# Perceiver layer on one core: self attention regrouped from one pair of heads per step to two pairs per stage

## The chip, the cores and the metric

One core of a Trainium2 chip runs the whole layer. The metric is device time in microseconds (us) of one execution. The kernel before takes 757.04 us, the median of three runs (756.72 to 757.04).

The engines are called as the profile calls them: PE (matmuls), PEld (weight loads for them), DVE and ACT (element by element work, both read the matmul results in PSUM), POOL (element by element work in SBUF) and SP (issues most DMAs). Each engine runs its own instructions in order; they wait for one another through semaphores.

## The reference

The layer is three residual blocks over x (256 tokens of 512):

```
x = x + cross_attention(layernorm(x), ctx_1024)      # 25088 context rows
x = x + self_attention(layernorm(x))                 # 16 heads of 64, one shared k and v, causal
x = x + mixture_of_experts(layernorm(x))             # 64 experts, 8 per token
```

The change touches the second block alone:

```
xn = layernorm(x);  q = xn w_q^T;  k, v = split(xn w_kv^T)
sim[h] = q[h] k^T * scale, masked causally;  attn[h] = softmax(sim[h])
out = concat_h(attn[h] v) w_out^T;  return layernorm(out)
```

Everything is 32 bit float.

## The kernel before

The 256 tokens are two tiles of 128 (`t`, `kt` = 0, 1; NT = 2). Width 512 is four chunks of 128 (ND = 4). The 16 heads are eight pairs `e` = 0..7 (NE = 8), because two heads of 64 fill 128 partitions. Cross attention takes the first 550 us or so, the experts begin at about 612 us; between them lies the self attention, of which the eight pairs take from 566.9 to 604.1 us.

What one pair needs:

- `queries(e)` (L907): eight matmul instructions (four chunks, two passes each) of 128x256 on all 128 rows and columns of the array, into a PSUM bank (`pa`), and one copy that scales the result into `aq`. The copy is on DVE for e = 1, 2, 3, otherwise on ACT (L925 to L928). For e = 0, 1 and half of 2 the queries lie before the loop.
- `scored(e)` (L998): eight matmul instructions for the scores `ps`. Each contracts 64 rows, the two heads side by side on the upper and lower half of the rows of the array. Then, on DVE, the causal mask is added (L1019, two additions) and the negated row maxima are found (L1023, two reductions).
- `exponential(e, t)` (L1027): ACT takes the exponential with the row sums, four activations for a pair, into `pe`.
- `divided(e, t)` (L1041): three reciprocals on DVE, three multiplications on POOL (L1049).
- `turned(e)` (L1055): six transposes on PE (`ptp`, on the whole array) and two copies out of PSUM: `pT0` (128x512, on DVE) and `pT1` (128x256, on ACT or DVE).
- `weighted(e)` (L1083): eight matmul instructions with 64 output columns each, the two heads on the left and right half of the columns of the array (`po`), and a copy of the result to `oT` on ACT. The last pair does this by halves of the tokens.
- `project` (L979): the output projection `pw`, two instructions of 128x512 for each token tile and pair, on the whole array. Some of them are used as fillers in the loop (`fill`).

So PE works in three arrangements of its array here: whole (queries, transposes, projection), two halves of rows (scores) and two halves of columns (products with the values).

The loop (L1123) is a pipeline over `e`: step e turns pair e - 2, divides pair e - 1, computes queries for a later pair (from step 6 on: two projections), scores pair e, weighs pair e - 2, and takes the exponentials of pair e. On PE a steady step is therefore transposes, queries, scores, products, each for one pair.

The order of the work is written out by hand: `in_turn` keeps the marked instructions of each engine in the order of the program. PSUM has eight banks. The two score tiles `ps` share four of them (`banks`, two buffers of two banks), so the scores of pair e + 2 wait until the exponentials of pair e have been read. `keys_bank`, `scores_bank`, `third_bank` and `apart` are one bank each; `among_three` goes round the first three of these.

After the loop the remaining projections follow (L1183 to L1189). When `pw` of the first token tile is complete, DVE and ACT compute its layer norms (`attended(0)`) while PE does six projections of the second tile.

Of the kernel before, what the change touches and what calls it, by code (L numbers as in the profile page):

```python
# [11 lines left out]
AF = mybir.ActivationFunctionType  # L12
# [3 lines left out]
P = 128  # L16
# [6 lines left out]
def tile_perceiver_layer(  # L23
# [25 lines left out]
    nc = tc.nc  # L49

    T, D = x.shape
# [3 lines left out]
    DH = a_wkvT.shape[1] // 2  # L55
# [4 lines left out]
    NT = T // P  # L60
    ND = D // P
# [4 lines left out]
    NE = INNER // P  # L66
# [26 lines left out]
    in_turn = tc.keep_in_program_order  # L93
# [112 lines left out]
    def keep_warm(*widths):  # L206
# [44 lines left out]
        fill=NEG,  # L251
# [269 lines left out]
    for i in range(2):  # L521
        t = cpool.tile([P, NT_SUMS, WIDTH + 2], F32, tag=f"T{i}", name=f"T_{i}", bufs=1)
# [125 lines left out]
    before, named = None, Named(0)  # L648
    for g in range(G):
# [25 lines left out]
        before, named = named, Named(g + 1)  # L675
# [26 lines left out]
    for line in RESULTS.strip().splitlines():  # L702
        to, x_, op, y_ = line.split()
        a_, b_, o_ = result(x_), result(y_), result(to)
        n = widths[to] = min(widths[x_], widths[y_])
        assert to not in ("c01", "c11") or n == WIDTH
        if to[0] == "c" and to[2] != "1":
            n = WIDTH - 2
        f = nc.vector.tensor_add if op == "+" else nc.vector.tensor_sub
# [78 lines left out]
    def among_three(name):  # L788
        turns[0] += 1
        return (keys_bank, scores_bank, third_bank)[turns[0] % 3](name)  # L790
# [113 lines left out]

    begun = {}

    def queries(e, lo=0, hi=T, where=apart, chunks=range(ND)):  # L907

        if chunks[0] == 0:
            begun[e, lo] = where(f"pa_{e}_{lo}")  # L910
        pa = begun[e, lo]
        for c in chunks:
            in_turn(
                nc.tensor.matmul(  # L914
                    pa[:, 0 : hi - lo],
                    lhsT=a_wqT_sb[:, c, e * P : (e + 1) * P],
                    rhs=anT[:, c, lo:hi],
                    start=(c == 0),
                    stop=(c == ND - 1),
                )  # L920
            )
        if chunks[-1] < ND - 1:
            return
        to, src = aq[:, e, lo:hi], pa[:, 0 : hi - lo]
        if 0 < e < 4:  # L925
            in_turn(nc.vector.tensor_scalar(to, src, 1.0 / DH, None, ALU.mult))
        else:
            in_turn(nc.scalar.activation(to, src, AF.Copy, scale=1.0 / DH))  # L928


    vT = hpool.tile([P, T], F32, tag="vT", name="vT")
# [62 lines left out]
    def fill(n):  # L994
        for _ in range(n):
            project(*fillers.pop(0))

    def scored(e):  # L998

        ps = banks(f"ps_{e}")  # L1000
        parts = []
        for t in range(NT):
            nk = (t + 1) * P
            lo = t * P
            parts.append(ps[:, :, lo : lo + nk])
            for i in range(2):
                half = slice(i * DH, (i + 1) * DH)
                in_turn(
                    nc.tensor.matmul(  # L1009
                        ps[:, i, lo : lo + nk],  # L1010
                        lhsT=aq[half, e, t * P : (t + 1) * P],
                        rhs=kk[half, 0:nk],
                        start=True,
                        stop=True,
                    )
                )
        for t, sc in enumerate(parts):
            diagonal = sc[:, :, t * P : (t + 1) * P]
            in_turn(nc.vector.tensor_add(diagonal, diagonal, tri))  # L1019
        maxima = []  # L1020
        for t, sc in enumerate(parts):
            nmx = small.tile([P, 2], F32, tag="nmx", name=f"nmx_{e}_{t}")
            in_turn(nc.vector.tensor_reduce(nmx, sc, AX.X, ALU.max, negate=True))  # L1023
            maxima.append(nmx)
        return parts, maxima, []

    def exponential(e, t):  # L1027
        parts, maxima, found = scores_of[e]
        nm = f"{e}_{t}"
        pe = work_b.tile([P, 2, (t + 1) * P], F32, tag=f"pe{t}", name=f"pe_{nm}", bufs=3)  # L1030
        sums = small.tile([P, 2, 1], F32, tag="sums", name=f"sums_{nm}")
        for i in range(2):
            in_turn(
                nc.scalar.activation(
                    pe[:, i, :], parts[t][:, i, :], AF.Exp, bias=maxima[t][:, i : i + 1],
                    accum_out=sums[:, i, :],
                )
            )
        found.append((pe, sums))

    def divided(e, t):  # L1041

        pe, sums = scores_of[e][2][t]
        rs = small.tile([P, 2, 1], F32, tag="rsm", name=f"rsm_{e}_{t}")

        n = 2 - t
        for i in range(0, 2, n):
            in_turn(nc.vector.reciprocal(rs[:, i : i + n], sums[:, i : i + n]))
            nc.gpsimd.tensor_mul(  # L1049
                pe[:, i : i + n],  # L1050
                pe[:, i : i + n],
                rs[:, i : i + n].to_broadcast([P, n, (t + 1) * P]),
            )

    def turned(e):  # L1055


        found = [pe for pe, _ in scores_of.pop(e)[2]]
        done = []
        pts = [among_three(f"ptp_{e}_{kt}") for kt in range(NT)]  # L1060

        for t, i, kt in ((0, 0, 0), (0, 1, 0), (1, 0, 0), (1, 0, 1), (1, 1, 0), (1, 1, 1)):
            o = i * (NT - kt) * P + (t - kt) * P
            in_turn(
                nc.tensor.transpose(  # L1065
                    pts[kt][:, o : o + P], found[t][:, i, kt * P : (kt + 1) * P], ident
                )
            )
        for kt, pt in enumerate(pts):
            n = (NT - kt) * P  # L1070
            pT = work_b.tile([P, 2, n], F32, tag=f"pT{kt}", name=f"pT_{e}_{kt}")
            to = pT.rearrange("p i q -> p (i q)")
            if kt == 1 and e < 2:

                copies_left.append((to, pt[:, : 2 * n]))
            elif kt == 0 or e == NE - 2:
                in_turn(nc.vector.tensor_copy(to, pt[:, : 2 * n]))
            else:
                in_turn(nc.scalar.copy(to, pt[:, : 2 * n]))
            done.append(pT)  # L1080
        return done

    def weighted(e, done):  # L1083


        if e == NE - 1:

            for t in range(NT):
                po = among_three(f"po_{e}_{t}")
                for kt in range(t + 1):  # L1090
                    for i in range(2):
                        in_turn(
                            nc.tensor.matmul(
                                po[i * DH : (i + 1) * DH, 0:P],
                                lhsT=va[:, kt, :],
                                rhs=done[kt][:, i, (t - kt) * P : (t - kt + 1) * P],
                                start=(kt == 0),
                                stop=(kt == t),
                            )
                        )  # L1100
                in_turn(nc.scalar.copy(oT[:, e, t * P : (t + 1) * P], po[:, 0:P]))
            return
        po = among_three(f"po_{e}")
        for kt, pT in enumerate(done):
            for i in range(2):
                in_turn(
                    nc.tensor.matmul(
                        po[i * DH : (i + 1) * DH, kt * P : T],
                        lhsT=va[:, kt, :],
                        rhs=pT[:, i, :],  # L1110
                        start=(kt == 0),
                        stop=(kt == NT - 1),
                    )
                )
        in_turn(nc.scalar.copy(oT[:, e, :], po[:, :T]))

    scores_of = {}
    copies_left = []  # L1120
    queries(1, P, T, where=among_three)
    turn_values()
    for e in range(NE + 2):  # L1123
        done = None
        if e == 1:
            queries(e + 1, P, T)
        if e == 2:
            queries(e + 2)
        if e == 3:
            queries(e + 2, chunks=range(ND // 2))  # L1130
        if e == NE + 1:
            fill(1)
        if e - 2 in scores_of:
            done = turned(e - 2)
        if e - 1 in scores_of:
            divided(e - 1, 0)
            for each in copies_left:
                in_turn(nc.vector.tensor_copy(*each))
            copies_left.clear()
            divided(e - 1, 1)  # L1140
        if e == 1:
            queries(e + 2, where=among_three)
        elif e == 3:
            queries(e + 2, chunks=range(ND // 2, ND))
        elif 2 < e < NE - 2:
            queries(e + 2)
        if e >= NE - 2:
            fill(2 if e <= NE else 1)
        if e < NE:
            scores_of[e] = scored(e)  # L1150
        if done is not None:
            weighted(e - 2, done)
        if e < NE:
            for t in range(NT):
                exponential(e, t)


    fn = work.tile([P, NT, D], F32, tag="tok", name="fn")
# [825 lines left out]
```

## Time and profile before

| what | us |
|---|---|
| median of three runs | 757.04 |
| the profiled execution's own time | 757.02 |
| its span, first to last instruction | 755.2 |
| PE busy in the span | 749.6 |
| the eight pairs, from the transposes of the values ahead of the first scores to the first projection behind the loop | 566.91 to 604.08 |
| the same stretch: DVE busy / ACT busy / POOL busy in 583.16 to 591.54 (8.38 long) | 5.96 / 5.25 / 3.51 |

The span is counted from the first to the last instruction; the 1.8 us by which the time exceeds it lie outside. Busy times of matmuls overlap, since each starts before the one ahead of it has ended; the distance from start to start tells what one costs. The granted PE clock is 1.00 of full speed in each stretch of the attention.

### The profile page before, as it was taken

The numbers are of one execution on the slowest core, as the hardware profiler recorded it, in microseconds if no ns is written. First come the engines' busy times: TensorE is split into PE (matmuls) and PEld (weight loads), VectorE is DVE, ScalarE is ACT, GpSimd is POOL, SyncE is SP. The second block draws the span as 40 slices with busy tenths as digits, with TensorE's granted clock in tenths as the row PEclk, the third lists the DMA queues.
The fourth block names the chain that finished last, engine by engine and source line by source line (L and its number), as shares of the span: only waits on it lengthen the run. The fifth ranks groups of instructions, "written<-read, shape, count | busy, mean of one in ns | idle before, by whom it ended". The sixth has DMA issues, their size and how long they took to land.

```text
span 755.2 us, 12461 instructions
## 1 busy us (share of the span) xinstructions
PE 749.6 (99%) x4046; PEld 614.8 (81%) x4046; DVE 571.6 (76%) x1644; ACT 200.9 (27%) x484; POOL 209.2 (28%) x402
## 2 busy tenths in 40 slices
PE   9999999999999999999999999999999999999998
PEld 6888888888888888888888888888977578876775
DVE  6988887888888788788878878888677669432465
ACT  4222222222222222222222222222244540001110
POOL 3222232232222223223222222322213315430461
PEclk9999999999999999999999999999999999999999
DMA  9999998997876887787788778774051007998552
GB/s 249 268 242 262 293 223 255 255 219 186 214 188 172 214 194 175 193 210 184 176 215 193 171 202 203 179 184 110 1 197 55 2 29 277 388 355 320 174 162 86
DMA packets 156147, 148.64 MB, mean 197 GB/s; under 512 B 8310, under 2 KB 113923, under 8 KB 156080
## 3 DMA queue, kind: packets, MB, share of 16 engines
q1 hardware_dynamic: 153168, 140.28, 70.5%
q0 software_dynamic: 2240, 7.02, 3.0%
q8 instruction: 33, 0.54, 0.3%
q10 hardware_dynamic: 672, 0.52, 0.2%
q14 instruction: 34, 0.28, 0.1%
HBM read 145.63 MB, written 2.16 MB: 196 GB/s over the span
## 4 chain that ended last, share of the span: by engine, by line
PE 99%; DVE 1%; ACT 0%; issue 0%
PE xacc L593 38%; PE pk L372 22%; PE pz L392 11%; PE ph_e L1263 7%; PE seven L1380 4%; PE pa L914 2%; PE ph_s L1263 2%; PE pw L983 2%; PE ph_few L1755 2%; PE po_few L1786 1%; PE ph_first L1263 1%; PE ph_second L1263 1%; PE pd_last L1448 1%; PE ptp L1065 1%; PE ps L1009 1%; PE py L757 1%
## 5 line engine op out<-in xcount | busy, mean ns | idle before, releaser
L593 PE MATMUL xacc<-T,S 128*128 128x172 f32 (+2 forms) x912 | 185.5, 308 | 0.0
L372 PE MATMUL pk<-cT,wkT_sb 128*128 128x384 f32 x512 | 175.5, 486 | 0.0
L593 PEld LDWEIGHTS xacc<-T,S 128*128 128x128 f32 x912 | 152.5, 190 | 20.1
L372 PEld LDWEIGHTS pk<-cT,wkT_sb 128*128 128x128 f32 x512 | 97.1, 190 | 54.4
L560 POOL TENSOR_TENSOR T<-ctx 128x172 f32<-128x172 f32 x65 | 31.8, 490 | 386.6 <-PE xacc L593 375.9
L336 DVE STREAM_TRANSPOSE cT<-quarters 128x1536 f32<-128x1536 f32 x64 | 113.5, 1774 | 0.5 <-issue 0.5
L560 DVE TENSOR_TENSOR T<-ctx 128x172 f32<-128x172 f32 (+1 forms) x262 | 113.5, 434 | 0.0
L560 DVE TENSOR_TENSOR S<-zT 128x128 f32<-128x128 f32 x196 | 57.1, 292 | 71.1 <-ACT zT L401 71.1
L392 PE MATMUL pz<-qT,kT 128*128 128x256 f32 x392 | 106.1, 379 | 0.0
L401 ACT ACTIVATE zT<-pz 128x256 f32<-128x256 f32 (+1 forms) x131 | 64.2, 490 | 113.7 <-PE pz L392 113.7
L593 PE MATMUL xacc<-T,zT 128*128 128x173 f32 (+1 forms) x396 | 89.9, 308 | 0.0
L593 PE MATMUL xacc<-ctx,S 128*128 128x172 f32 x392 | 78.5, 309 | 0.0
L383 ACT ACTIVATE kT<-pk,bk 128x384 f32<-128x384 f32 (+2 forms) x68 | 38.4, 568 | 146.8 <-PE pk L372 146.8
L560 DVE TENSOR_TENSOR S<-zT,S 128x128 f32<-128x128 f32 x325 | 76.6, 285 | 0.0
L570 ACT COPY T<-ctx 128x170 f32<-128x170 f32 (+1 forms) x130 | 43.2, 334 | 124.9 <-PE xacc L593 120.6
L560 POOL TENSOR_TENSOR T<-ctx,T 128x170 f32<-128x170 f32 (+1 forms) x130 | 72.4, 574 | 0.0
L560 DVE TENSOR_TENSOR T<-ctx,T 128x172 f32<-128x172 f32 x195 | 65.4, 361 | 8.2 <-PE xacc L593 1.5
L392 PEld LDWEIGHTS pz<-qT,kT 128*128 128x128 f32 x392 | 68.5, 190 | 3.8 <-ACT kT L383 0.2
L593 PEld LDWEIGHTS xacc<-T,zT 128*128 128x128 f32 x396 | 66.4, 190 | 0.3
L593 PEld LDWEIGHTS xacc<-ctx,S 128*128 128x128 f32 x392 | 62.8, 190 | 0.1
L593 PE MATMUL xacc<-ctx,zT 128*128 128x170 f32 (+1 forms) x264 | 59.5, 307 | 0.0
L1263 PE MATMUL ph_e<-fT,gu 128*128 128x256 f32 x224 | 50.3, 381 | 0.0
(310 smaller groups left out, 791.4 us busy)
## 6 DMA issues: line engine op xcount, KB each, us to landing
ctx<-in_context SPq DMA_DIRECT2D x65, 768.0 KB, 5.3
quarters<-in_context SPq DMA_DIRECT2D x256, 192.0 KB, 6.4
gu<-in_e_gate_up SPq DMA_DIRECT2D x12, 1024.0 KB, 8.1
gu_s<-in_s_gate_up SPq DMA_DIRECT2D x8, 512.0 KB, 6.5
dn<-in_e_down SPq DMA_DIRECT2D x7, 512.0 KB, 6.8
a_wqT<-in_a_wqT SPq DMA_DIRECT2D x4, 512.0 KB, 7.5
a_wout<-in_a_woutT SPq DMA_DIRECT2D x1, 2048.0 KB, 10.4
dn_s<-in_s_down SPq DMA_DIRECT2D x4, 512.0 KB, 8.8
```

Of the source, the lines that this page charges most:

```text
L336: in_turn(nc.vector.transpose(new_turned(g), q.rearrange("p b (c r) -> p c b r", r=R)))
L372: nc.tensor.matmul(pk, lhsT=w[:, c, :], rhs=cT[:, c, 0 : n // R, :].rearrange("p b r -> p (b r)"), start=(c == 0), stop=(c == ND - 1),)
L383: in_turn(nc.scalar.activation(kT[:, lo:hi], pk[:, lo:hi], AF.Identity, bias=bk_sb))
L392: nc.tensor.matmul(pz[:, i * T : (i + 1) * T], lhsT=kT[:, at : at + P], rhs=qT, start=True, stop=True,)
L401: nc.scalar.activation(zT[:, blocks[0] : blocks[-1] + 1, :].rearrange("p j t -> p (j t)"), pz[:, 0 : len(blocks) * T], AF.Sigmoid, scale=1 ...
L560: in_turn(f(o_, a_, b_))
L570: in_turn(nc.scalar.copy(named[to][:, 0:n], named[x_][:, 0:n]))
L593: nc.tensor.matmul(banks_of_products[i][:, cols], lhsT=named[lhs], rhs=named[rhs][:, 0:n],  start=i not in opened, stop=(g == G - 1 and last),
L914: nc.tensor.matmul(pa[:, 0 : hi - lo], lhsT=a_wqT_sb[:, c, e * P : (e + 1) * P], rhs=anT[:, c, lo:hi], start=(c == 0), stop=(c == ND - 1),)
L983: nc.tensor.matmul(pw[t], lhsT=oT[:, e, t * P : (t + 1) * P], rhs=a_wout_sb[:, e, :], start=(e == 0), stop=(e == NE - 1),)
L1263: nc.tensor.matmul(ph[:, f * T + lo : f * T + hi], lhsT=gu[:, c, col : col + P], rhs=fT[:, c, lo:hi], start=(c == 0), stop=(c == ND - 1),)
L1380: nc.tensor.matmul(product_of_seven(nm), lhsT=block(n, hT, dn, s_, t_, lhs), rhs=block(n, hT, dn, s_, t_, rhs),  start=(n == SEVEN[0] and ...
```

## The change

The loop goes over stages `d` = 0..4 instead of steps. A stage scores two pairs, 2d and 2d + 1, one behind the other; then it turns the first pair of the stage before, computes queries (or projections), turns the second pair of the stage before, computes queries again, and forms the products with the values for both of these pairs, one behind the other. The amount of matmul work is the same.

- `queries` is split: the matmuls, and `queries_copied`, which is placed later. In the loop the copies are all on ACT; before, those for e = 2 (second half) and 3 were on DVE.
- `scored` is split: the matmuls, and `masked`, the masks and maxima on DVE.
- `turned` is told which banks to use and which copies are ACT's (`by_act`). `pT1` is always ACT's (before, for e = 0, 1 and 6, DVE's), and for e = 1, 3 and 5 `pT0` is ACT's as well.
- `weighted` is told its banks; the copy to `oT` is split off (`output_copied`) and placed behind the exponentials of the stage's second pair.
- The divisions of the first pair are in its own stage, those of the second pair at the end of the stage.
- Seven projections are in the loop as fillers instead of eight; the eighth follows behind it.
- Fixed banks take the place of `among_three` in the loop.

```diff
-        if 0 < e < 4:
-            in_turn(nc.vector.tensor_scalar(to, src, 1.0 / DH, None, ALU.mult))
-        else:
-            in_turn(nc.scalar.activation(to, src, AF.Copy, scale=1.0 / DH))
+        if by_act:
+            in_turn(nc.scalar.activation(to, src, AF.Copy, scale=1.0 / DH))
+        else:
+            in_turn(nc.vector.tensor_scalar(to, src, 1.0 / DH, None, ALU.mult))
...
+    half = ND // 2
+    queries_of = (
+        ([(2, P, T, keys_bank), (3, 0, T, apart)], [(4, 0, T, third_bank)]),
+        ([(5, 0, T, apart)], [(6, 0, T, keys_bank, range(half))]),
+        ([(6, 0, T, keys_bank, range(half, ND))], [(7, 0, T, apart)]),
+    )
+
+    def ahead(d, j):
+        if d < len(queries_of):
+            for e, lo, hi, *where in queries_of[d][j]:
+                chunks = where[1] if len(where) > 1 else range(ND)
+                queries(e, lo, hi, where[0], chunks, copied=False)
+        elif d == len(queries_of):
+            fill(2)
+        else:
+            fill(2 - j)
...
+    for d in range(NE // 2 + 1):
+        now = [e for e in (2 * d, 2 * d + 1) if e < NE]
+        before = (2 * d - 2, 2 * d - 1) if d else ()
+        free = apart if d == 2 else keys_bank
+        done = {}
+        for e in now:
+            scored(e)
+        if now:
+            masked(now[0])
+        if before:
+            done[before[0]] = turned(before[0], (free, scores_bank), (1,))
+        if now and not before:
+            exponential(now[0], 0)
+            exponential(now[0], 1)
+            ahead(d, 0)
+            masked(now[1])
+            divided(now[0], 0)
+            divided(now[0], 1)
+            ahead_copied(d, 0)
+            ahead(d, 1)
+        else:
+            for t in range(NT if now else 0):
+                exponential(now[0], t)
+            ahead(d, 0)
+            if now:
+                masked(now[1])
+                divided(now[0], 0)
+                divided(now[0], 1)
+            done[before[1]] = turned(
+                before[1], (third_bank, scores_bank), (0, 1) if now else (1,)
+            )
+            ahead_copied(d, 0)
+            ahead(d, 1)
+            weighted(before[0], done[before[0]], third_bank)
+            if now:
+                weighted(before[1], done[before[1]], scores_bank)
+            else:
+                output_copied(before[0])
+                weighted(before[1], done[before[1]], scores_bank, keys_bank)
+        if now:
             for t in range(NT):
-                exponential(e, t)
+                exponential(now[1], t)
+            ahead_copied(d, 1)
+            for e in before:
+                output_copied(e)
+            divided(now[1], 0)
+            divided(now[1], 1)
```

More of the change, by code (lines that the diff above doesn't have):

```diff
@@ L905, in tile_perceiver_layer, with queries @@
     begun = {}
-    def queries(e, lo=0, hi=T, where=apart, chunks=range(ND)):
+    def queries(e, lo=0, hi=T, where=apart, chunks=range(ND), copied=True):
         if chunks[0] == 0:
@@ L921, in queries, with queries_copied @@
             )
-        if chunks[-1] < ND - 1:
-            return
-        to, src = aq[:, e, lo:hi], pa[:, 0 : hi - lo]
-        if 0 < e < 4:
+        if chunks[-1] == ND - 1 and copied:
+            queries_copied(e, lo, hi, by_act=e == 0)
+    def queries_copied(e, lo=0, hi=T, by_act=True):
+        to, src = aq[:, e, lo:hi], begun.pop((e, lo))[:, 0 : hi - lo]
+        if by_act:
+            in_turn(nc.scalar.activation(to, src, AF.Copy, scale=1.0 / DH))
+        else:
             in_turn(nc.vector.tensor_scalar(to, src, 1.0 / DH, None, ALU.mult))
-        else:
-            in_turn(nc.scalar.activation(to, src, AF.Copy, scale=1.0 / DH))
     vT = hpool.tile([P, T], F32, tag="vT", name="vT")
@@ L1016, in scored, with masked @@
                 )
+        scores_of[e] = parts, [], []
+    def masked(e):
+        parts, maxima, _ = scores_of[e]
         for t, sc in enumerate(parts):
@@ L1019, in scored @@
             in_turn(nc.vector.tensor_add(diagonal, diagonal, tri))
-        maxima = []
         for t, sc in enumerate(parts):
@@ L1024, in scored @@
             maxima.append(nmx)
-        return parts, maxima, []
     def exponential(e, t):
@@ L1053, in divided, with turned @@
             )
-    def turned(e):
+    def turned(e, where, by_act):
         found = [pe for pe, _ in scores_of.pop(e)[2]]
         done = []
-        pts = [among_three(f"ptp_{e}_{kt}") for kt in range(NT)]
+        pts = [where[kt](f"ptp_{e}_{kt}") for kt in range(NT)]
         for t, i, kt in ((0, 0, 0), (0, 1, 0), (1, 0, 0), (1, 0, 1), (1, 1, 0), (1, 1, 1)):
@@ L1072, in turned, with weighted @@
             to = pT.rearrange("p i q -> p (i q)")
-            if kt == 1 and e < 2:
-                copies_left.append((to, pt[:, : 2 * n]))
-            elif kt == 0 or e == NE - 2:
+            if kt in by_act:
+                in_turn(nc.scalar.copy(to, pt[:, : 2 * n]))
+            else:
                 in_turn(nc.vector.tensor_copy(to, pt[:, : 2 * n]))
-            else:
-                in_turn(nc.scalar.copy(to, pt[:, : 2 * n]))
             done.append(pT)
         return done
-    def weighted(e, done):
-        if e == NE - 1:
+    def weighted(e, done, *where):
+        if len(where) == NT:
             for t in range(NT):
-                po = among_three(f"po_{e}_{t}")
+                po = where[t](f"po_{e}_{t}")
                 for kt in range(t + 1):
@@ L1102, in weighted @@
             return
-        po = among_three(f"po_{e}")
+        po = where[0](f"po_{e}")
         for kt, pT in enumerate(done):
@@ L1114, in weighted, with output_copied @@
                 )
-        in_turn(nc.scalar.copy(oT[:, e, :], po[:, :T]))
+        outputs[e] = po
+    def output_copied(e):
+        in_turn(nc.scalar.copy(oT[:, e, :], outputs.pop(e)[:, :T]))
+    outputs = {}
     scores_of = {}
-    copies_left = []
     queries(1, P, T, where=among_three)
     turn_values()
[L1123 to L1153, printed above, removed]
-            for t in range(NT):
-                exponential(e, t)
@@ new lines, in ahead_copied @@
+    def ahead_copied(d, j):
+        if d < len(queries_of):
+            for e, lo, hi, *where in queries_of[d][j]:
+                if len(where) == 1 or where[1][-1] == ND - 1:
+                    queries_copied(e, lo, hi)
+    for d in range(NE // 2 + 1):
[34 more added lines that the diff above has]
+                weighted(before[1], done[before[1]], scores_bank)
+            else:
+                output_copied(before[0])
+                weighted(before[1], done[before[1]], scores_bank, keys_bank)
+        if now:
+            for t in range(NT):
+                exponential(now[1], t)
[4 more added lines that the diff above has]
+            divided(now[1], 1)
```

## The prediction

> **What bounds it now.** I read the page first, its chain that ended last and the busy times, then the stretch of the eight pairs: busy times window by window, the order of time on PE, on ACT and on DVE.
>
> ```profile
> PE 749.6 (99%) x4046; PEld 614.8 (81%) x4046; DVE 571.6 (76%) x1644; ACT 200.9 (27%) x484; POOL 209.2 (28%) x402
> PE 99%; DVE 1%; ACT 0%; issue 0%
> 574.14:578.87 4.73, 4.50 (x32) 2.96 (x31) 3.94 (x11) 3.02 (x15) 1.76 (x3) 1.00 0.01 3
> 578.87:583.16 4.29, 4.29 (x31) 3.03 (x30) 3.33 (x10) 2.77 (x14) 1.75 (x3) 1.00 0.01 2
> 587.36:591.54 4.18, 4.18 (x28) 2.30 (x27) 2.98 (x8) 2.63 (x13) 1.75 (x3) 1.00 0.00 0
> ```
>
> The first two lines are the page's: PE is the whole chain. The others are steps of the loop, from one pair's first score to the next one's: length, then busy us of PE, PEld, DVE, ACT, POOL, the granted clock, DMA. A steady step is 4.18 (PE full, ACT 2.63, DVE 2.98, no DMA). The steps from 574.14 and 578.87 hold the same PE work and take 0.55 and 0.11 more: waits. So only PE time can be won: by fewer waits, or by cheaper matmuls. The second is in the order of time on PE (start, length, instructions, count):
>
> ```profile
> 586.83 0.59 PE L914 MATMUL pa<-anT,a_wqT 128*128 128x256 f32 x2
> 587.05 0.38 PE L914 MATMUL pa<-anT,a_wqT 128*128 128x256 f32 x1
> 587.36 0.38 PE L1009 MATMUL ps<-kk,aq 64*128 64x128 f32 x2
> 587.68 0.60 PE L1009 MATMUL ps<-kk,aq 64*128 64x256 f32 x4
> 587.90 0.38 PE L1009 MATMUL ps<-kk,aq 64*128 64x256 f32 x2
> 588.21 0.44 PE L1107 MATMUL po<-pT,va 128*64 128x256 f32 x2
> 588.48 0.49 PE L1107 MATMUL po<-pT,va 128*64 128x256 f32 x4
> 588.80 0.28 PE L1107 MATMUL po<-pT,va 128*64 128x128 f32 x2
> 589.01 0.33 PE L1065 MATMUL ptp<-ident,pe 128*128 128x128 f32 x1
> 589.18 0.49 PE L1065 MATMUL ptp<-ident,pe 128*128 128x128 f32 x3
> ```
>
> Read starts, not lengths. 256 wide matmuls follow at 0.22 (586.83, 587.05; 587.68, 587.90), 128 wide ones at 0.11. Whenever the arrangement of the array changes (128*128, 64*128, 128*64), the last instruction before lasts 0.09 to 0.10 longer (587.05 to 587.36 is 0.31; 587.90 to 588.21 is 0.31; 588.80 to 589.01 is 0.21), and the first one after also: scores 0.10 (587.36 to 587.68 is 0.32 for two that need 0.22), products 0.05 (588.21 to 588.48), transposes 0.06 (589.01 to 589.18), other whole-array matmuls 0.10 (604.08 to 604.61). A steady pair pays three changes: 0.09+0.10+0.09+0.05+0.10+0.06 = 0.49 of its 4.18.
>
> **The change, part by part.**
>
> *Two pairs side by side.* Changes in the loop before: whole to rows 8, rows to whole 2, rows to columns 6, columns to whole 8, whole to columns 2: 26. After: stage 0 into and out of the scores 2; stages 1 to 3 each into scores, out to transposes, into products 9; out of the products of stage 3, into and out of those of stage 4, 3: 14. Leaving: 26 x 0.095 = 2.47 becomes 1.33. Entering scores: 8 x 0.10 becomes 4; entering columns: 8 x 0.05 becomes 4; entering whole: 5 x 0.06 and 5 x 0.10 become 4 x 0.06 and 2 x 0.10. Together 4.47 becomes 2.37: **-2.1**. Columns straight to rows is not in the trace; between 0.14 and 0.20 a change, I take 0.195, as whole to rows costs.
>
> [...]
>
> *Old waits of PE.* The excess of the two early steps, 0.55+0.11, less 0.04 for a dearer entry (queries behind products instead of transposes): **-0.6**. They are waits for `pT1` and `aq` 4, queued behind exponentials, and for POOL. After, stage 1's products come four microseconds behind its transposes, and nothing waits there.
>
> *The copies moved to ACT, and the copies placed later.* No PE time of their own; hidden if ACT keeps up. Its rows:
>
> ```profile
> 588.33 0.90 DVE L1019 TENSOR_TENSOR ps<-ps,tri 128x256 f32<-128x256 f32 x2 [0.20 <-PE ps L1009]
> 589.26 1.02 DVE L1023 TENSOR_REDUCE nmx<-ps 128x2 f32<-128x256 f32 x2
> 590.40 0.37 ACT L1034 ACTIVATE pe<-ps,nmx 128x128 f32<-128x128 f32 x1 [0.90 <-DVE nmx L1023]
> 592.00 0.38 ACT L1079 COPY pT<-ptp 128x256 f32<-128x256 f32 x1
> 610.83 0.59 ACT L308 COPY fT<-pt_fn 128x512 f32<-128x512 f32 x1 [1.75 <-PE pt_fn L298]
> ```
>
> Masks and maxima of a pair take 1.95 (588.33 to 590.28), 0.12 later its exponentials start and hold ACT 1.60 (590.40 to 592.00; last sum at 592.12). ACT is idle 0.90 before them.
>
> What is late next is the second pair's score bank: it is free only after that pair's exponentials, and these stand on ACT behind the first pair's exponentials and three copies. The ring, exponentials of one second pair to those of the next: reciprocal 0.27 (they stand on DVE ahead of the next masks), masks 1.95, 0.12, exponentials 1.60, `pT0` on ACT 0.59 (the only 128x512 copy of ACT is `fT`), `pT1` 0.26, one `aq` 0.29, exponentials 1.72: **6.8**. PE's stage: two steady pairs less one set of changes, 8.38 - 0.49 = 7.89 in stage 3; stages 1 and 2 hold 12 query instructions instead of 16, 0.86 less: 7.03. So ACT is hidden by 0.2 at the tightest, and by 1.1 in stage 3.
>
> *New waits.* In stage 0 there is no cover. Placed on the times of before: masks of pair 0 end at 569.95, those of pair 1 at 571.8; the exponentials of pair 0 end at 571.76, then `aq` 2 and 3 (0.2+0.29), so those of pair 1 run from 572.2 to 573.95. PE: scores of pair 1 end at 568.5, queries 2 (half), 3, 4 take 0.9+0.1+1.73+1.73, so scores 2 start at 573.05, scores 3 could at 573.9: wait 0.1. In stage 4 the transposes of pair 6 use the scores bank, free after the copy of `oT` 5, which stands behind the last exponentials: 0.2. Scores 7 wait for `aq` 7, copied behind the exponentials of pair 5: just in time. Bounds: 0.1 (only stage 0), and 1.2 if every handover to scores 3, 5, 7 is 0.3 later. I take **+0.3**.
>
> *Moved work.* The eighth filler projection goes behind the loop, same PE time; it covers the copy of `oT` 7. Six projections still cover `attended(0)` (fn is done at 609.86, PE turns it at 610.19). No DMA is issued in the loop, so SP passes nothing. Division of second pairs: POOL's 1.75 must end 3.9 later, before the second transposes; covered by the scores, transposes and queries between.
>
> **Sum.** -2.1 - 0.6 + 0.3 = -2.4 in the pairs' 37.2. Behind them PE is busy 131.7 of 135.0, and what feeds it follows from the routing, which comes 2.4 earlier as well; so it passes to the end. The profiled execution goes from 757.02 (span 755.2) to 754.6; the median shown, 757.04, is the same within 0.02: **754.6**.
>
> **Rivals.**
>
> 1. *The changes cost what they cost* (no saving): the loss belongs to the first weights of each block, not to the array's arrangement, and comes again between the two pairs' blocks. For: each block has its own stationary operand. Against: within a block of scores or products weights change as well, without loss. Then -0.6+0.3: 756.7. 12%.
> 2. *Slower, ACT and DVE as the bound.* [...] The place: the ring above. Each us that it exceeds PE's stage is paid at scores 3, 5 and 7. From (2.4 + 0.3) / 3 = 0.9 on nothing is left of the gain, from 1.4 per handover the kernel is over 1.5 slower; at 1.7 it is 759.4. Against: ACT is busy 5.25 of 8.38 now, and with `pT0` 5.84 of 7.0. 8%.
> 3. *Part of the gain eaten*: the 0.2 of cover is gone and each handover waits 0.4, or the experts' stage gives some back: 755.9. 12%.
>
> **Numbers.** My forecast has 68%, with its own range 753.9 to 755.5 (new waits 0.1 to 1.2). A measurement can tell 0.2%, 1.5 us, from no change: faster is below 755.5. Faster: 0.68 and a third of rival 3, 0.72; within: 0.18; slower: 0.10, rival 2 and what I haven't seen. The range leaves out rival 2 and the edges: 753.8 to 756.8.
>
> **What would show it.** PE's order of time: scores of two pairs joined at 0.21, without 0.31; 14 changes. PE's waits: one of about 0.1 at scores 3, one at the transposes of pair 6. Loop end near 601.7 instead of 604.08. Wrong if scores 5 or 7 wait for exponentials by over 0.5, if the joint of two score blocks costs 0.2, or if the experts' stage is longer than before.

## The result, and the profile after

The kernel after takes 754.78 us (median of 9 runs, 754.40 to 755.27) against 756.90 (9 runs): a ratio of 0.9971, 95% interval 0.9961 to 0.9981, so faster by 2.1 us, 0.3%. 754.6 was forecast.

The page of the kernel after, line 1 and the chain that ended last:

```profile
PE 746.8 (99%) x4046; PEld 615.0 (82%) x4046; DVE 566.2 (75%) x1636; ACT 203.0 (27%) x492; POOL 208.5 (28%) x402
PE 98%; DVE 1%; DMA 0%; ACT 0%; issue 0%
```

PE is still the chain, with the same 4046 matmuls, and it is busy 2.8 us less. None was taken away, so they follow one another sooner. How much of that is cheaper changes of the arrangement and how much shorter waits, the starts tell.

The stages 1, 2 and 3, from the first score of a stage to what follows its products (length, then busy us of PE, PEld, DVE, ACT, POOL, granted clock, DMA):

```profile
572.90:580.04 7.14, 7.14 (x58) 5.46 (x57) 4.98 (x16) 5.40 (x24) 3.94 (x8) 1.00 0.01 2
580.04:587.06 7.02, 7.02 (x59) 5.54 (x57) 4.97 (x15) 5.31 (x23) 3.29 (x7) 1.00 0.01 2
587.06:594.98 7.92, 7.92 (x55) 4.69 (x53) 5.29 (x17) 6.13 (x25) 4.37 (x9) 1.00 0.01 3
```

7.03, 7.03 and 7.89 were forecast. ACT is busier in a stage than before (5.3 of 7.0), but not full.

The order of time on PE where stage 2 begins (start, length, instructions, count). Neighbouring windows of the trace overlap, so a line may repeat an instruction of the one above; read the starts:

```profile
579.83 0.28 PE L1108 MATMUL po<-pT,va 128*64 128x128 f32 x2
580.04 0.38 PE L1012 MATMUL ps<-kk,aq 64*128 64x128 f32 x2
580.36 0.60 PE L1012 MATMUL ps<-kk,aq 64*128 64x256 f32 x4
580.58 0.49 PE L1012 MATMUL ps<-kk,aq 64*128 64x256 f32 x4
581.02 0.60 PE L1012 MATMUL ps<-kk,aq 64*128 64x256 f32 x4
581.24 0.38 PE L1012 MATMUL ps<-kk,aq 64*128 64x256 f32 x2
581.55 0.33 PE L1070 MATMUL ptp<-ident,pe 128*128 128x128 f32 x1
```

Columns to rows, which the trace before didn't have, costs what was taken for it: 579.83 to 580.04 is 0.21 where 0.11 would do, and 580.04 to 580.36 is 0.32 for two that need 0.22. Eight instructions of pair 4 and eight of pair 5 follow without a break: from 580.58 to 581.02 there are one 256 wide step (0.22) and two 128 wide ones (0.11 each), the joint of the two pairs among them, and nothing is added. Only at the end of both, 581.24 to 581.55, is the 0.09 paid once.

For what follows, one measure is better than the whole time: **the stretch of the pairs**, from the transposes of the values to the transposes of the normalized tokens. It is 43.28 before (566.91 to 610.19) and 40.93 after (566.73 to 607.66): -2.35. From its end to the last matmul both kernels take 141.17, and the instructions there are the same in the same order on every engine. So the gain goes through undiminished. (The medians differ by 2.12, in a repeat below by 2.40; the stretch is the sharper figure, as the last section shows.)

### The profile page after: what moved, and what is told of

Its sections match the earlier page's. It is cut to its first block, busy times and chain, and to the rows that moved or that the text cites. A ratio compares the mean times of both kernels' runs of the same rounds, so it can differ in the third digit from the quotient of the medians.

```text
span 752.7 us, 12458 instructions
## 1 busy us (share of the span) xinstructions
PE 746.8 (99%) x4046; PEld 615.0 (82%) x4046; DVE 566.2 (75%) x1636; ACT 203.0 (27%) x492; POOL 208.5 (28%) x402
## 4 chain that ended last, share of the span: by engine, by line
PE 98%; DVE 1%; DMA 0%; ACT 0%; issue 0%
PE xacc L593 38%; PE pk L372 22%; PE pz L392 11%; PE ph_e L1304 7%; PE seven L1421 4%; PE ph_s L1304 2%; PE pa L914 2%; PE ph_few L1796 2%; PE pw L986 2%; PE po_few L1827 1%; PE ph_first L1304 1%; PE ph_second L1304 1%; PE pd_last L1489 1%; PE ps L1012 1%; PE ptp L1070 1%; PE py L757 1%
```

## The experiments

Each run undoes or adds one part of the account. The indented text is what was expected of it; times are medians, and +1.01 and the like are differences of the stretch from that of the kernel that was edited (after: 40.93; before: 43.28).

**Scores apart.** Undoes one part: the second pair's scores stand alone again.

```diff
-        for e in now:
+        for e in now[: 1 if before else 2]:
             scored(e)
...
             done[before[0]] = turned(before[0], (free, scores_bank), (1,))
+            for e in now[1:]:
+                scored(e)
```

> The kernel after, with the scores of a stage's second pair moved behind the transposes of the first pair of the stage before (stages 1 to 3). The matmuls are the same, the changes of the array's arrangement go from 14 to 20. Theory (each change costs what its rows show): a stage pays whole to rows once more (0.095 leaving, 0.10 entering) and rows to whole once more with the dearer entry (0.095, 0.10): 0.39 a stage, three stages 1.17, less the 0.06 that scores 7 wait for now: +1.1 us over the kernel after, 755.9. Rival (the loss belongs to the first weights of each block, whatever its neighbour): both kernels have the same blocks, so no difference, 754.8.

Measured: 755.64, stretch 41.94, +1.01. PE's order of time in stage 2 of this kernel:

```profile
580.56 0.93 PE L1012 MATMUL ps<-kk,aq 64*128 64x128 f32 x8
581.42 0.87 PE L1070 MATMUL ptp<-ident,pe 128*128 128x128 f32 x6
582.22 0.93 PE L1012 MATMUL ps<-kk,aq 64*128 64x128 f32 x8
583.08 1.13 PE L914 MATMUL pa<-anT,a_wqT 128*128 128x256 f32 x4
```

Each block of scores takes 0.86 to the next start, where the joined 16 of the kernel after take 1.51 together. The same blocks with the same first weights cost 1.0 more once a block of another arrangement stands between them: the rival that charges the first weights of every block, whatever stands before it, falls. (In what form the first weights do come in is told in the last section.) The waits at scores 3 (0.12) and scores 7 (0.06) are gone here, so the six changes cost 1.01 + 0.18 = 1.19, where 1.17 was worked out; the expectation had left out the first of these waits.

**Products apart too.** In stage 2 a chunk of queries, in stage 3 a projection stands between the two pairs' products.

```diff
-            ahead(d, 1)
+            if d == 2:
+                queries(7, 0, T, apart, range(ND - 1), copied=False)
+            elif d == 3:
+                fill(1)
+            else:
+                ahead(d, 1)
             weighted(before[0], done[before[0]], third_bank)
+            if d == 2:
+                queries(7, 0, T, apart, range(ND - 1, ND), copied=False)
+            elif d == 3:
+                fill(1)
```

> As the run with the scores apart, and in stages 2 and 3 a chunk of queries or a projection stands between the products of the two pairs. 24 changes. Theory: two stages more with columns to whole (0.095+0.10) and whole to columns (0.095+0.05), 0.34 each, so +0.7 on top of +1.1: +1.8 over the kernel after, 756.6, most of the change's gain gone. A wait of the first products for a copy of the turned weights may add up to 0.3 in stage 2. Rival (first weights of a block): 754.8 plus that wait.

Measured: 756.30, stretch 42.63, +0.69 on top of the run before (0.68 expected), +1.70 in all.

```profile
586.12 0.87 PE L1108 MATMUL po<-pT,va 128*64 128x256 f32 x8
586.92 0.70 PE L914 MATMUL pa<-anT,a_wqT 128*128 128x256 f32 x2
587.55 0.87 PE L1108 MATMUL po<-pT,va 128*64 128x256 f32 x8
```

Two query instructions, 0.43 elsewhere, take 0.63 to the next start here. With 24 changes instead of 14 most of the gain is gone (0.65 of 2.35 is left); ten changes cost 1.19 + 0.69 = 1.88, 0.19 each. That is the main term, measured by putting it back.

**Copies on DVE.** The turned blocks of pairs 1, 3, 5 are copied by DVE, as before.

```diff
-                before[1], (third_bank, scores_bank), (0, 1) if now else (1,)
+                before[1], (third_bank, scores_bank), (1,)
```

> The kernel after, with the copies of the first turned block of pairs 1, 3 and 5 on DVE again instead of ACT. The rival that ACT is nearly the bound: ACT gains 0.47 a stage, so -0.1 or nothing. Theory: DVE does these copies behind the reciprocals of the stage's first pair, which end at 578.5, 585.6 and 592.6; with 0.68 for the copy the bank for the first products is free at about 579.2, 586.3, 593.3, where PE comes at 578.6, 585.6, 593.5: waits of 0.65, 0.75 and 0, so +1.4 over the kernel after, 756.2.

Measured: 755.66, stretch 42.07, +1.14. DVE and PE in stage 1:

```profile
578.36 0.67 DVE L1081 COPY pT<-ptp 128x512 f32<-128x512 f32 x1
579.09 1.52 PE L1108 MATMUL po<-pT,va 128*64 128x256 f32 x16 [0.46 <-DVE pT L1081]
```

PE waits for the copy, which stands behind masks and reciprocals on DVE. The products come 0.54 late in stage 1 and 0.66 more in stage 2; 0.65 and 0.75 were expected, because DVE started the copy at 578.36 instead of 578.5. Scores 7 gain their 0.06. So the move to ACT is no detail: half of the gain hangs on these three copies. It is more a matter of DVE's order than of its load: DVE works without a longer break from the masks at 573.83 to the end of this copy, and is then idle for 2.0 of the 2.5 us until the next masks. An earlier place for the copy on DVE was not tried.

**A dose on ACT.** Two copies whose result nobody uses ("idle" below), ahead of the second pair's exponentials in stages 1 to 3.

```diff
+            for i in range(2 if before else 0):
+                dose = work_b.tile([P, D], F32, tag="dose", name=f"dose_{d}_{i}")
+                in_turn(nc.scalar.copy(dose, x1[:, i, :]))
             for t in range(NT):
                 exponential(now[1], t)
```

> The kernel after with two idle copies of 128x512 on ACT (0.47 each from start to start, 0.94 a stage) ahead of the exponentials of the second pair in stages 1, 2 and 3. The ring as predicted (6.8) becomes 7.74 against PE stages of 7.03, 7.03 and 7.89: theory +0.7 at scores 5 and +0.9 at scores 7 (which wait for nothing but just so now), and in stage 4 the transposes of pair 6 wait 0.6 longer for the copy of oT 5: +2.2 over the kernel after, 757.0, between +1.6 and +2.6. If ACT had more cover than the ring says, under +1.0; if ACT were already the bound, 3 x 0.94 = +2.8.

Measured: 756.58, stretch 43.03, +2.10.

```profile
581.38 0.93 PE L1012 MATMUL ps<-kk,aq 64*128 64x128 f32 x8 [0.60 <-ACT pe L1039]
589.22 0.93 PE L1012 MATMUL ps<-kk,aq 64*128 64x128 f32 x8 [0.56 <-ACT aq L929]
597.42 0.55 PE L1070 MATMUL ptp<-ident,pe 128*128 128x128 f32 x3 [0.45 <-ACT oT L1119]
```

The three waits come at the three places that were named: scores 5, scores 7, and the transposes of pair 6 behind `oT` 5. They lengthen PE's order by 0.88, 0.77 and 0.45 (0.7, 0.9, 0.6 expected, for a dose of 0.94; it was 1.03 a stage, 0.515 a copy). So the ring of ACT and DVE lies just below PE: of a dose of 1.03, 0.15 is hidden at scores 5. At scores 7, 0.26 is hidden, because the exponentials of pair 4 start only 0.60 later than in the kernel after (from the start of the stretch), while PE is 0.88 late by then. Slower by ACT was a real case, and not far off: a us more on ACT per stage takes nine tenths of the gain.

**One old wait alone.** In the kernel before, the copy of queries 4 on DVE.

```diff
-        if 0 < e < 4:
+        if 0 < e < 5:
```

> The kernel before, with one thing changed: the copy of queries 4 is on DVE instead of ACT, where it stood behind the exponentials of pair 1 and kept queries 5 out of their bank. Measures one of the old waits alone. Theory: of the 0.6 of old waits this is the one of queries 5, with the weight load behind it 0.23 to 0.35: the step from the scores of pair 2 to those of pair 3 falls from 4.73 to about 4.45; the wait of the products for the second turned block stays (0.2). The whole: -0.25 against before, 756.65. If the old waits were hidden anyway: 756.9.

Measured: 756.97 against 756.99, stretch 43.27 against 43.28: nothing. PE and POOL in this kernel:

```profile
575.60 1.13 PE L914 MATMUL pa<-anT,a_wqT 128*128 128x256 f32 x4
579.84 1.28 PE L1065 MATMUL ptp<-ident,pe 128*128 128x128 f32 x6
578.87 1.75 POOL L1049 TENSOR_TENSOR pe<-pe,rsm 128x256 f32<-128x256 f32 x3 [2.18 <-DVE rsm L1048]
```

Counted from the start of the stretch, queries 5 begin at 9.07 instead of 9.37: that wait went as expected. But the transposes of pair 2, 4.2 later, now take 1.11 to the next start instead of 0.82: they wait for POOL's division of pair 2, which ends at 580.62. The 0.30 came back one place on, so the 0.25 that was expected of the whole did not come.

**More cover for that chain.** As before, and half of queries 6 ahead of the transposes of pair 2.

```diff
-        if 0 < e < 4:
+        if 0 < e < 5:
...
-        if e == 3:
+        if e in (3, 4):
             queries(e + 2, chunks=range(ND // 2))
...
-        elif e == 3:
+        elif e in (3, 4):
             queries(e + 2, chunks=range(ND // 2, ND))
```

> The run before, the copy of queries 4 on DVE, took 0.30 from one wait and gave it back at the transposes of pair 2, which waited for the division of that pair. Here half of queries 6 is also put ahead of those transposes (as queries 5 already are ahead of those of pair 1), in the kernel before. Theory: the old waits are the chain of pair 2, from its scores to its divided weights, 6.9 long, which had too little PE work beside it; with 0.86 more cover the 0.29 at the transposes goes and nothing takes its place: the pairs' stretch to the first transposes of the normalized tokens falls from 43.28 to about 42.9, 756.6. If the wait only moves on again (to the scores of pair 4 or 5): 43.25, 756.9.

Measured: 756.85 against 757.03 (the difference is within its interval), stretch 43.05, -0.23; 42.9 was expected.

```profile
584.84 0.99 PE L1065 MATMUL ptp<-ident,pe 128*128 128x128 f32 x6
```

The transposes of pair 2 no longer wait, but those of pair 3, shown here, take 0.83 instead of 0.71, and queries behind products enter at 0.10 instead of 0.06. So part of the old waits can be had without the change, in pieces; the last of them moves on by a pair each time. With the run before it this says that they belong to the chain from a pair's scores to its divided weights more than to one copy.

**The new waits taken away.** In the kernel after, three more query copies on DVE, and other banks in stage 4.

```diff
-                    queries_copied(e, lo, hi)
+                    queries_copied(e, lo, hi, by_act=e not in (2, 3, 7))
...
-            done[before[0]] = turned(before[0], (free, scores_bank), (1,))
+            done[before[0]] = turned(
+                before[0], (free, scores_bank if now else third_bank), (1,)
+            )
...
-                before[1], (third_bank, scores_bank), (0, 1) if now else (1,)
+                before[1],
+                (third_bank, scores_bank) if now else (scores_bank, third_bank),
+                (0, 1) if now else (1,),
...
-            weighted(before[0], done[before[0]], third_bank)
+            weighted(before[0], done[before[0]], third_bank if now else keys_bank)
...
-                weighted(before[1], done[before[1]], scores_bank, keys_bank)
+                weighted(before[1], done[before[1]], scores_bank, third_bank)
```

> The kernel after without its three new waits: the copies of queries 2, 3 and 7 are on DVE, and in stage 4 the transposes of pair 6 use the bank of the products of pair 4 instead of that of pair 5, the following banks moved round accordingly. In the trace of the kernel after, scores 3 lose 0.12, scores 7 0.06 and the transposes of pair 6 0.21. Theory: -0.35 to -0.4 against the kernel after, 754.4, the pairs' stretch 34.5 instead of 34.9. Rival (a wait taken away comes back at the next place, since the ring of ACT and DVE has only 0.2 of cover): no gain, 754.8.

Measured: 754.22, stretch 40.53, -0.40.

```profile
572.72 1.58 PE L1012 MATMUL ps<-kk,aq 64*128 64x128 f32 x16
594.62 0.87 PE L1070 MATMUL ptp<-ident,pe 128*128 128x128 f32 x6
```

The 16 scores of stage 1 take 1.58 instead of 1.70, the transposes of pair 6 0.87 instead of 1.09; nothing came back elsewhere. (The 34.5 and 34.9 of the expectation end the stretch at 601.65, where the last fourteen projection instructions before the transposes begin.) Both kernels again, on one chip:

> The kernel after, unchanged, on the same chip as the next run, to compare with it: stretch 40.93, 754.8, 2.1 to 2.2 below before.

> The kernel after without its three new waits, unchanged from its first run: stretch 40.53, 0.40 below the kernel after on the same chip, 754.3 to 754.4.

Measured: 754.63 (stretch 40.95) and 754.36 (stretch 40.53), ratios to before 0.9969 (0.9957 to 0.9981) and 0.9965 (0.9951 to 0.9979). By the trace the second is 0.4 shorter each time; by the whole time the two can't be told apart.

## Why the prediction was right

- *Two pairs side by side, -2.1*: right in size and cause. The price per change by the rows held where it is paid again (1.19 for six, 0.69 for four), also for columns to rows, which had to be taken from a neighbour. Putting back ten of the twelve changes that were saved cost 1.88.
- *Old waits, -0.6*: right in size. -2.35 with 2.10 saved and 0.39 lost leaves 0.64, and the order of time on PE in the kernel before shows most of it at two places:

```profile
575.26 0.69 PE L1107 MATMUL po<-pT,va 128*64 128x256 f32 x4
575.62 0.44 PE L1107 MATMUL po<-pT,va 128*64 128x128 f32 x4
576.28 0.48 PE L914 MATMUL pa<-anT,a_wqT 128*128 128x256 f32 x1 [0.23 <-ACT aq L928]
```

  From 575.26 to 575.62 is 0.36 and from there to 576.28 is 0.66, where an undisturbed pair (from 588.48 on) takes 0.22 and 0.32: about 0.5 lost, before the second turned block of pair 0 and before queries 5. The transposes of pair 2 lose another 0.11. But the sentence that laid these waits to single copies was too simple: without the wait for `aq` 4 nothing was won.
- *New waits, +0.3*: 0.39, at the places named. The order of time on PE in the kernel after, at the first of them and at the largest:

```profile
573.44 0.61 PE L1012 MATMUL ps<-kk,aq 64*128 64x256 f32 x4
573.68 0.71 PE L1012 MATMUL ps<-kk,aq 64*128 64x128 f32 x6
574.00 0.39 PE L1012 MATMUL ps<-kk,aq 64*128 64x256 f32 x2
...
595.25 0.59 PE L1070 MATMUL ptp<-ident,pe 128*128 128x128 f32 x2
595.52 0.44 PE L1070 MATMUL ptp<-ident,pe 128*128 128x128 f32 x2
```

  The transpose at 595.25 is followed after 0.27 instead of 0.11, when `oT` 5 has left the bank, and the one after that is late by 0.055 as well: 0.21 together. At scores 3 (573.68) the wait is 0.02, but from there to 574.00 two 128 wide steps take 0.32 where the joint of stage 2 (580.58 to 581.02) has 0.22 for them: 0.12 together. At scores 7 it is 0.06 in all.
- *The ring, 6.8 against 7.03*: right that it is hidden, and by little. In stage 2, ACT and DVE:

```profile
581.01 0.90 DVE L1026 TENSOR_TENSOR ps<-ps,tri 128x256 f32<-128x256 f32 x2 [0.34 <-PE ps L1012]
583.09 0.37 ACT L1039 ACTIVATE pe<-ps,nmx 128x128 f32<-128x128 f32 x1 [0.20 <-DVE nmx L1029]
584.68 0.87 ACT L1079 COPY pT<-ptp 128x512 f32<-128x512 f32 x2
585.41 0.42 ACT L929 ACTIVATE aq<-pa 128x256 f32<-128x256 f32 x1
585.69 0.41 ACT L1039 ACTIVATE pe<-ps,nmx 128x128 f32<-128x128 f32 x1
587.27 0.45 ACT L929 ACTIVATE aq<-pa 128x256 f32<-128x256 f32 x1
```

  The ring as it was summed has more cover than 0.2: DVE waits 0.34 for PE's scores before it masks pair 4. The two turned copies take 0.73 from start to start, not 0.85 (the 0.59 for `pT0` was a busy length; to the next start it costs 0.47), and the exponentials of a second pair 1.58, not 1.72 (585.69 to 587.27). What is tight is the part of it inside a stage, from PE's scores of the first pair on: from 583.09 on ACT has no idle time until the copy of queries 7. The cover was measured as 0.15 at scores 5; scores 7 have none, since they wait for `aq` 7 already. That 0.15 came so near to 0.2 is in part luck.
- *Moved work and DMA*: right, the projection behind the loop took the dearer entry (0.10) off the next one, and the part behind the stretch is 141.17 in every kernel. The loop's end near 601.7 holds if it is read as the start of the fourteen projection instructions that stand behind the loop in both kernels: 601.65. The eighth filler stands ahead of them now, from 600.68 on.

## What to carry to other kernels

When PE is full, read starts, not busy times: a change between whole, row halves and column halves costs 0.14 to 0.20 us here, on both sides of the change, and grouping blocks of one arrangement saves it without a matmul less. Then look for the ring of the other engines that the new grouping must fit under, and count its cover per stage: here it is 0.0 to 0.2 us, and three copies that stood behind other work on their engine cost 1.1. A wait taken out of a pipeline is worth only what the chain behind it can pass on: one wait of 0.30 in the kernel before gave nothing, the three new ones of the kernel after gave all of their 0.40.

## What was not expected of the hardware

- The dearer entry isn't paid only at a change of arrangement. After a mere wait, within one arrangement, the second instruction is late as well: 0.10 at scores 3 and 0.055 at the transposes of pair 6, the same amounts as after a change. So at these two places a short wait on PE costs itself and that. What the two cases have in common shows in the weight loads (PEld): inside a block, in the kernel after; at a change, in the kernel before; behind a wait, in the kernel after.

```profile
580.81 0.30 PEld L1012 LDWEIGHTS ps<-kk,aq 64*128 64x128 f32 x3
587.36 0.52 PEld L1009 LDWEIGHTS ps<-kk,aq 64*128 64x128 f32 x8 [0.33 <-issue]
595.52 0.31 PEld L1070 LDWEIGHTS ptp<-ident,pe 128*128 128x128 f32 x3 [0.23 <-ACT oT L1119]
```

  Inside a block a load starts with the matmul ahead of its own, here 0.11 early: the one at 580.81 is for the matmul that starts at 580.91. At a change and behind a wait, PEld stands idle (0.33, 0.23), and the first load starts together with its matmul (587.36, 595.52) instead of 0.11 ahead of it. The dearer entries also go with the length of these first loads: 0.13 for products and 0.14 for transposes, which enter at 0.05 and 0.06; 0.18 for scores and 0.19 for projections, which enter at 0.10. So the entry half of the price seems to be the first weights after all, as the first rival had it, but only where the arrangement changes or PE waits. That is read from the rows, no run varied the loads alone; and what the 0.09 on leaving consists of stays open.
- The stretch repeats within 0.02 us between profiles of one kernel (40.93 and 40.95; 40.53 twice), while its start wandered from 566.53 to 567.31 over eleven profiles of nine kernels, with the same instructions ahead of it. What moves the start was not tried. A gain of 0.4 in one stage is seen in that stage long before it is seen in the whole time.
